# Fewer, smaller products for k and v, and the edits that came with them, in a one-core RWKV and routed-FFN layer

## The chip, the core and the metric

The kernel runs on one core of a Trainium2 chip. The metric is the device time of one execution in microseconds (us). The engines are named as the profile names them: PE is TensorE (its weight loads are PEld), DVE is VectorE, ACT is ScalarE, POOL is GpSimd, SP is SyncE, which only starts DMAs here. Each engine runs its own instructions in the order in which they were issued; semaphores make one wait for another.

## The reference

```python
xn = layernorm(x)                                  # x: [1, 2048, 512]
r, v, k = split(xn @ W_rvk.T)                      # three of [2048, 512]
# per channel, w = -exp(time_decay), u = time_first, over the tokens in order:
#   no = max(o, u+k);  A = exp(o-no);  B = exp(u+k-no);  y = (A*p + B*v) / (A*q + B)
#   no2 = max(w+o, k); p, q, o = exp(w+o-no2)*p + exp(k-no2)*v, exp(w+o-no2)*q + exp(k-no2), no2
attn = (sigmoid(r) * y) @ W_out.T
probs = softmax(xn @ classifier.T)                 # 12 experts: 8 routed, 4 that return their input
idx = top_2(probs + bias);  w_full = one_hot(idx) * probs * 1.5
ffn = sum over e < 8 of w_full[e] * down_e(silu(gate_e xn) * up_e xn)  +  xn * sum of w_full[8:]
out = x + attn + ffn
```

All of it is fp32. gate and up are [256, 512] for each expert, down is [512, 256].

## The kernel before

Tokens are handled in 4 blocks of 512 (`NTB`, `TB`), channels in 4 chunks of 128 (`CC`). A block and a chunk, (b, c), make a unit, 16 in all.

**The head.** For each block the tokens are normalized (`norm`), stored to HBM as `xs`, turned by PE into `xnT` with channels on the partitions (`turn_block`), and multiplied by the classifier (`logits`, `add_quarters`). Then DVE works through the routing: it picks the two experts of each token, counts tokens per expert with one-hot matmuls (`pc`), gives each a slot in one of 23 tiles of 128 tokens (two of which mix experts in groups of 32), and builds one-hot tables in bf16: `lowhot` (L548, the place within a tile), `hh` (L555, the tile) and `tok` (L562, `hh` times the five values carried for each token). 32 matmuls of these tables (`pi`, L570) give the list of tokens and weights of every tile. While DVE does that, `fill(n)` issues n product steps on PE; before the tables these are 9 and 18, between the two halves 7, after them 2, 3, 4 and 5. The tables and all routing buffers stay allocated to the end of the kernel.

**The products.** `project(b, c)` (L270 to L291) computes k, v and r of a unit in turn: four fp32 matmuls of 128 x 128 by 128 x 512 each into one PSUM buffer of `ps_mm` (two buffers), one step per matmul; then ACT copies k or v to SBUF (L289), or takes exp of -r (L287). The first two units (`all_products`) go name by name.

**The recurrence.** `scan(b, c)` (L293 to L336) has four stages. Stage 0, DVE: the first column of `obv` from the state (L304), a running maximum (L308), two differences (L310, L311). Stage 1, ACT: two exponentials (L313, L314). Stage 2, DVE: two running sums and a product (L320 to L322), then numerator and denominator (L326 to L329). Stage 3: POOL copies the last column of `obv` into the channel's state (L332), ACT that of `sums` (L333), DVE takes the reciprocal (L334) and multiplies into `yT` (L335). The buffers `obv` and `a2` come from `wk`, which has two of each; `sums` and `den` from `wk1`, with one.

**The expert tiles.** For tile i POOL gathers 128 rows of `xs` (`gather`, L642); `flip` copies them on ACT as 16-bit halves (L709), a DMA on SP's queue transposes them, `unite` puts the halves together on ACT (L717); `turn` (L697) is the other way, four PE transposes and one ACT copy, used only for tiles beyond the 23. Then gate and up on PE (`up`), tanh on ACT and two DVE operations (`activate`), the turned activation, the down product (`finish`) into `ps_o`, scaled by ACT into `yo` (L770), and a scatter on POOL's queue that adds the 128 rows to `out` in HBM (L774). Each such accumulating DMA waits until the one before has landed. SP fetches the weights (1 MB for gate and up, 0.5 MB for down).

**The attention output.** `attention(b, [j])` multiplies 128 tokens of `yT` by W_out (L875), into `ps_tr` for the first rows; DVE adds the share of the input-returning experts (L887), and POOL's queue adds the row block to `out` (L890). The last blocks go through `read_out` instead, which reads `out` back, adds (L845, L884, L871) and stores.

**The order.** After the head the order is a table: `plan(at, generator)` gives each step a due time in nominal microseconds, and the steps are issued in order of due time. Units of the recurrence are planned every `UNIT` = 19.0, with stages at 0, 4, 6 and 12; product steps in groups of four; `after` names the groups in whose place a piece of attention stands; a tile has a first half (up, activate, gather of the tile after next but one) and a second half. The very end is the attention of the last two blocks.

Of the kernel before, what the change touches and what calls it, by code (L numbers as in the profile page):

```python
# [26 lines left out]
F32 = mybir.dt.float32  # L27
BF16 = mybir.dt.bfloat16
I32 = mybir.dt.int32
U16 = mybir.dt.uint16  # L30
AF = mybir.ActivationFunctionType
# [4 lines left out]
P = 128  # L36
T = 2048
C = 512
# [17 lines left out]
MAX_TILES = 40  # L56
FAR = 8192.0
NV = 5
QW = 32


@with_exitstack
def layer(ctx: ExitStack, tc: tile.TileContext, x, w_rvk, w_out, decay, first, cls, ebias, gu, down, out):
    nc = tc.nc

    def pool(name, bufs, **kw):
        return ctx.enter_context(tc.tile_pool(name=name, bufs=bufs, **kw))
# [3 lines left out]
    xyp = pool("xy", 5)  # L71
    ewp = pool("ew", 3)
    gathered = pool("gathered", 2)
    wk1 = pool("wk1", 1)
    rows = pool("rows", 3)
    basep = pool("base", 4)
    rp = pool("route", 1)
    small = pool("small", 2)
    kvp = pool("kv", 5)
    erp = pool("er", 4)  # L80
    wk = pool("wk", 2)
    ex_p = pool("exp", 2)
    dram = pool("dram", 1, space=bass.MemoryType.DRAM)
    ps_mm = pool("ps_mm", 2, space=bass.MemoryType.PSUM)
    ps_gu = pool("ps_gu", 2, space=bass.MemoryType.PSUM)
    ps_o = pool("ps_o", 2, space=bass.MemoryType.PSUM)
    ps_tr = pool("ps_tr", 2, space=bass.MemoryType.PSUM)

    xs = dram.tile([T, C], F32, tag="xs", name="xs")

# [77 lines left out]
        nc.gpsimd.tensor_copy(t, i32)  # L168
        return t

    lane = iota([P], [[1, P]], 0, "lane", BF16)
    tiles128 = iota([MAX_TILES], [[P, MAX_TILES]], 0, "tiles128", BF16)
    tiles_f = iota([MAX_TILES], [[P, MAX_TILES]], 0, "tiles_f", F32)
    number = iota([MIXED], [[1, MIXED]], 0, "number", F32, 1)
    expert = iota([E], [[1, E]], 0, "expert", F32)
    tok_j = iota([2, NT], [[0, 2], [1, NT]], 0, "tok_j", BF16, 1)
    tok_p = iota([1], [[0, 1]], 1, "tok_p", F32)
    spare = iota([2], [[0, 2]], 1, "spare", F32, T + P)
    vals = rp.tile([P, 2, NT, NV], BF16, tag="vals", name="vals")
    nc.gpsimd.tensor_copy(vals[:, :, :, 0], tok_j)  # L180
    nc.gpsimd.tensor_copy(vals[:, :, :, 1], tok_p.unsqueeze(1).to_broadcast([P, 2, NT]))
    one8 = rp.tile([P, E], F32, tag="one8", name="one8")
    nc.gpsimd.memset(one8, 1.0)
    hotb = rp.tile([P, NT + 1, E], BF16, tag="hotb", name="hotb")
# [108 lines left out]
    def scan(b, c):  # L293

        n = f"{b}_{c}"
        s = state[c]
        w, cf = wdec[:, c : c + 1], cfac[:, c : c + 1]
        k = kvr[b, c, "k"]
        if c == 0:
            yT[b] = xyp.tile([P, CC, TB], F32, tag="xy", name=f"yT{b}")  # L300


        obv = wk.tile([P, 3, TB + 1], F32, tag="obv", name=f"obv{n}")
        nc.vector.tensor_copy(obv[:, :, 0:1], s[:, 0:3].unsqueeze(2))  # L304
        o, bs, bvs = (obv[:, m, 0:TB] for m in range(3))
        o2, b2, bv = (obv[:, m, 1 : TB + 1] for m in range(3))

        nc.vector.tensor_tensor_scan(o2, w.to_broadcast([P, TB]), k, s[:, 0:1], ALU.add, ALU.max)  # L308
        a2 = wk.tile([P, TB], F32, tag="a2", name=f"a2{n}")
        nc.vector.scalar_tensor_tensor(a2, o, w, o2, ALU.add, ALU.subtract)  # L310
        nc.vector.tensor_sub(b2, k, o2)  # L311
        yield
        nc.scalar.activation(a2, a2, AF.Exp)  # L313
        nc.scalar.activation(b2, b2, AF.Exp)  # L314
        yield

        v = kvr[b, c, "v"]
        sums = wk1.tile([P, 2, TB], F32, tag="sums", name=f"sums{n}")
        sq, sp = sums[:, 0, :], sums[:, 1, :]
        nc.vector.tensor_tensor_scan(sq, bs, a2, s[:, 3:4], ALU.add, ALU.mult)  # L320
        nc.vector.tensor_mul(bv, b2, v)
        nc.vector.tensor_tensor_scan(sp, bvs, a2, s[:, 4:5], ALU.add, ALU.mult)  # L322

        er = kvr[b, c, "r"]
        den = wk1.tile([P, TB], F32, tag="den", name=f"den{n}")
        nc.vector.scalar_tensor_tensor(den, b2, cf, sq, ALU.mult, ALU.add)  # L326
        nc.vector.scalar_tensor_tensor(den, er, 1.0, den, ALU.add, ALU.mult)
        num = wk.tile([P, TB], F32, tag="a2", name=f"num{n}")
        nc.vector.scalar_tensor_tensor(num, bv, cf, sp, ALU.mult, ALU.add)  # L329
        yield  # L330
        if b + 1 < NTB:
            nc.gpsimd.tensor_copy(s[:, 0:3].unsqueeze(2), obv[:, :, TB : TB + 1])  # L332
            nc.scalar.copy(s[:, 3:5].unsqueeze(2), sums[:, :, TB - 1 : TB])  # L333
        nc.vector.reciprocal(den, den)  # L334
        nc.vector.tensor_mul(yT[b][:, c, :], num, den)  # L335
        yield  # L336

    units = [(b, c) for b in range(NTB) for c in range(CC)]
    LEAD = 4

    def whole(gen):
        for _ in gen:
# [1 line left out]

    def all_products():
        for name, m in (("k", 2), ("v", 1), ("r", 0)):
            for u in range(2):
                yield from project(*units[u], ((name, m),))
        for u in range(2, len(units)):
            yield from project(*units[u])  # L350

    products = all_products()

    def fill(n):
        for _ in range(n):
            next(products, None)


    manual = ExitStack()
    manual.enter_context(tc.manual_schedule())  # L360
# [7 lines left out]
    for b in range(NTB):  # L368
        if b + 1 < NTB:
            norm(b + 1)  # L370
        fill(1 if b else 2)
        logits(b)
        fill(1 if b else 3)
        if b + 1 < NTB:
            turn_block(b + 1)
        add_quarters(b)
# [73 lines left out]
    nc.vector.tensor_reduce(wts, hot[:, :, :, :E], AX.X, ALU.add)  # L450
    nc.vector.tensor_scalar_mul(wts, wts, 0.5 * SCALE)

    for n in range(3):
        nc.vector.tensor_copy(vals[:, :, :, 2 + n], wts)
        if n < 2:
            nc.vector.tensor_sub(wts, wts, vals[:, :, :, 2 + n])

    def narrow8(tag, dt=F32):
        return rp.tile([P, E], dt, tag=tag, name=tag)

# [77 lines left out]


    NK = 2 * NT
    lowhot = xyp.tile([P, NK, P], BF16, tag="xy", name="lowhot")
    pi = ps_o.tile([P, NV, MAX_TILES], F32, tag="o", name="pi")
    fill(18)
    for m in range(2):
        ks = slice(m * NT, (m + 1) * NT)
        nc.vector.tensor_tensor(  # L548
            lowhot[:, ks, :],
            lane.unsqueeze(1).to_broadcast([P, NT, P]),  # L550
            low[:, m].unsqueeze(2).to_broadcast([P, NT, P]),
            ALU.is_equal,
        )
        hh = rp.tile([P, NT, MAX_TILES], BF16, tag="hh", name=f"hh{m}")
        nc.vector.tensor_tensor(  # L555
            hh,
            tiles128.unsqueeze(1).to_broadcast([P, NT, MAX_TILES]),
            high_b[:, m].unsqueeze(2).to_broadcast([P, NT, MAX_TILES]),
            ALU.is_equal,
        )  # L560
        tok = ewp.tile([P, NT, NV, MAX_TILES], BF16, tag="gw", name=f"tok{m}")
        nc.vector.tensor_tensor(  # L562
            tok,
            hh.unsqueeze(2).to_broadcast([P, NT, NV, MAX_TILES]),
            vals[:, m].unsqueeze(3).to_broadcast([P, NT, NV, MAX_TILES]),
            ALU.mult,
        )
        for j in range(NT):
            k = m * NT + j
            nc.tensor.matmul(pi, lowhot[:, k, :], tok[:, j], start=(k == 0), stop=(k == NK - 1))  # L570
        if m == 0:
            which_i = place_tiles()
            fill(7)
    nc.vector.tensor_scalar_mul(wdec, wdec, -1.0)
    cfac = const.tile([P, CC], F32, tag="cfac", name="cfac")
    nc.vector.tensor_add(cfac, first_sb, wdec)
# [272 lines left out]
    def attention(b, js=range(NJ)):  # L849

        for j in js:
            i = b * NJ + j
            if i < (NTB - 2) * NJ - 2:
                po = ps_tr.tile([P, C], F32, tag="tr", name=f"pw{i}")
            elif j >= 2 if i in orows else j % 2 == 1:
                po = ps_mm.tile([P, C], F32, tag="mm", name=f"pw{i}")
            else:
                po = ps_o.tile([P, C], F32, tag="o", name=f"pw{i}")
# [31 lines left out]
                nc.gpsimd.dma_start(out[i * P : (i + 1) * P, :], xrows[i], accum_op=ALU.add)  # L890


    gather(0)
    gather(1)
    for i in range(2):
# [1 line left out]
        fetch_down(i)  # L897
        fetched["w"] += 1
        fetched["d"] += 1
    fill(2)  # L900
    stages = [scan(*u) for u in units]
    next(stages[0])
    fill(3)
    next(stages[0])
    fill(4)
    next(stages[0])
    flip(0)
    flip(1)
    fill(5)
    next(stages[0])  # L910
    gather(2)
    unite(0)

    UNIT = 19.0
    after = {12: (0, 0), 13: (0, 1), 18: (0, 2), 19: (0, 3), 32: (1, 0), 33: (1, 1), 40: (1, 2), 41: (1, 3)}
    groups = 3 * (len(units) - LEAD) - 2 + len(after)  # L920
    total = groups * 3.43 + TILES * 5.2
    table = []

    def plan(at, what, *args):
        table.append((at, iter([(what, *args)]) if args else what))

    for u in range(1, len(units)):
        for at in (0, 4, 6, 12):
            plan((u - 1) * UNIT - 7 + at, stages[u])
    one = total / groups / CC  # L930
    for m in range(groups):
        if m in after:
            b, j = after[m]
            group = attention(b, [j])
            plan(CC * m * one - 16, read_xn, b, [j])

            plan(CC * (m + 2 - j % 2) * one + 1, group)
        else:
            group = products
        for k in range(CC):  # L940
            plan((CC * m + k) * one, group)


    spread = (total - 12) / TILES
# [83 lines left out]
```

## Time and profile before

| | |
|---|---|
| median of 3 runs | 379.0 us (377.15 to 381.65) |
| profiled execution | 379.6 us, span 377.8 us |
| PE busy | 369.5 us, 98% |
| DVE busy | 273.2 us, 72% |
| ACT, POOL busy | 161.4 us (43%), 95.3 us (25%) |
| granted PE clock, mean | 0.995 |
| DMA | 87.37 MB, mean 231 GB/s |

The page divides the span into 40 slices; each digit is the busy share of an engine in tenths, 9 standing for 90% or more. A row of groups has line, engine, operation, out<-in, sizes, count, then busy us, mean ns of one, and the idle time of the engine just before such instructions with what ended it. Matmuls are pipelined, and each record contains the fill of the array, so records overlap and busy PE time is less than the sum of the records. An fp32 matmul leaves two matmul records and two weight loads. A line of the timeline has start, duration, engine, line and operation; the bracket at its end is the idle time before it and what ended that.

The head's fixed points in the timeline: the last logits at 37.3, counts `pc` at 45.1, `lowhot` from 54.62, the first `tok` until 61.2, `pi` until 70.2, the token list at 71.24, the first expert product at 85.6. PE's last matmul ends at 374.27.

### The profile page before, as it was taken

To read this page: it belongs to the slowest core of one execution; us is meant where nothing else is said; L and a number is where in the kernel's file an instruction comes from. 1 tells how busy PE (TensorE), PEld (TensorE's weight loads), DVE (VectorE), ACT (ScalarE), POOL (GpSimd) and SP (SyncE) were. 2 spreads that over 40 slices of the span, in tenths; PEclk is the share of its full clock that TensorE was granted. 3 is DMA by queue.
4 is the path that set the end of the run, shared out by engine and by line. 5 is a ranking of instruction groups with operands and counts; after the bars stand their busy time and mean duration, and the time that the engine had idled before them with its cause. 6 is when DMAs were issued, how large, how long until landed. Compare 5 with 4: busy or idle time off the path is not lost. (4 is left out here: it accounts for less than half of the span.)

```text
span 377.8 us, 3672 instructions
## 1 busy us (share of the span) xinstructions
PE 369.5 (98%) x1076; PEld 167.0 (44%) x1076; DVE 273.2 (72%) x420; ACT 161.4 (43%) x266; POOL 95.3 (25%) x131
## 2 busy tenths in 40 slices
PE   7999999999999999999999999999999999999996
PEld 2565444534443443434434444444444444434443
DVE  4872889899995887556957685929593779379905
ACT  1676211153455555535454655445642644432000
POOL 5000300231123322221332333424122311322520
PEclk9899999999999999999999999999999999999999
DMA  7998941835878799999999899799999698774494
GB/s 275 404 360 303 334 141 61 320 77 157 177 214 222 164 335 282 314 271 316 240 208 302 236 244 289 158 248 356 209 246 267 154 320 165 155 249 56 58 205 158
DMA packets 59605, 87.37 MB, mean 231 GB/s; under 512 B 38976, under 2 KB 39360, under 8 KB 55808
## 3 DMA queue, kind: packets, MB, share of 16 engines
q1 hardware_dynamic: 52272, 67.07, 59.8%
q0 software_dynamic: 7312, 20.06, 24.7%
q8 instruction: 9, 0.15, 0.2%
q14 instruction: 12, 0.10, 0.1%
HBM read 63.25 MB, written 19.27 MB: 218 GB/s over the span
## 5 line engine op out<-in xcount | busy, mean ns | idle before, releaser
L684 PE MATMUL pg<-gw,xgT 128*128 128x512 f32 x168 | 75.8, 593 | 0.0
L774 POOL DMA_INDIRECT out_dram<-yo,to_i x23 | 39.0, 1697 | 133.9 <-ACT yo L770 55.8
L276 PE MATMUL pk<-xnT,wrvk 128*128 128x512 f32 x128 | 60.7, 598 | 0.5 <-ACT v L289 0.5
L276 PE MATMUL pr<-xnT,wrvk 128*128 128x512 f32 x128 | 59.8, 593 | 0.0
L276 PE MATMUL pv<-xnT,wrvk 128*128 128x512 f32 x128 | 59.6, 596 | 0.0
L875 PE MATMUL pw<-wout_sb,yT 128*128 128x512 f32 x120 | 54.0, 594 | 0.1
L334 DVE RECIPROCAL den<-den 128x512 f32<-128x512 f32 x16 | 53.5, 3345 | 0.0
L684 PEld LDWEIGHTS pg<-gw,xgT 128*128 128x128 f32 x168 | 31.8, 190 | 40.1 <-issue 37.5
L736 DVE SCALAR_TENSOR_TENSOR th<-th,pg 128x256 f32<-128x256 f32 x23 | 9.6, 419 | 54.8 <-ACT th L735 54.8
L684 PE MATMUL po<-dw,actT 128*128 128x512 f32 x84 | 39.6, 593 | 0.8 <-ACT yo L770 0.8
L276 PEld LDWEIGHTS pv<-xnT,wrvk 128*128 128x128 f32 x128 | 23.9, 190 | 30.7 <-issue 29.2
L276 PEld LDWEIGHTS pk<-xnT,wrvk 128*128 128x128 f32 x128 | 23.9, 192 | 30.6 <-issue 29.1
L276 PEld LDWEIGHTS pr<-xnT,wrvk 128*128 128x128 f32 x128 | 24.1, 190 | 30.0 <-issue 29.5
L875 PEld LDWEIGHTS pw<-wout_sb,yT 128*128 128x128 f32 x120 | 22.6, 190 | 28.6 <-issue 28.6
L642 POOL DMA_INDIRECT xg<-xs,token_i x23 | 24.4, 1059 | 40.3 <-DMA gw<-in_gu_dram 30.2
L735 ACT ACTIVATE th<-pg 128x256 f32<-128x256 f32 x23 | 8.8, 383 | 54.0 <-PE pg L684 46.7
L320 DVE TENSOR_TENSOR_SCAN sums<-obv,state,a 128x512 f32<-128x512 f32 x16 | 20.5, 1282 | 12.8 <-ACT obv L314 12.8
L709 ACT COPY xp<-xg 128x1024 uint16<-128x1024 uint16 x23 | 24.0, 1045 | 6.7 <-DMA xq<-xp 3.7
L717 ACT COPY xgT<-xq 128x1024 uint16<-128x1024 uint16 x23 | 26.7, 1159 | 0.0
L684 PEld LDWEIGHTS po<-dw,actT 128*128 128x128 f32 x84 | 15.9, 190 | 21.2 <-issue 19.1
L770 ACT ACTIVATE yo<-po,wplace 128x512 f32<-128x512 f32 x23 | 15.8, 685 | 19.5 <-PE po L684 19.4
L322 DVE TENSOR_TENSOR_SCAN sums<-obv,state,a 128x512 f32<-128x512 f32 x16 | 20.6, 1284 | 0.6
(195 smaller groups left out, 389.9 us busy)
## 6 DMA issues: line engine op xcount, KB each, us to landing
gw<-in_gu_dram SPq DMA_DIRECT2D x25, 1024.0 KB, 7.9
dw<-in_down_dram SPq DMA_DIRECT2D x25, 512.0 KB, 4.5
x<-in_x_dram SPq DMA_DIRECT2D x16, 256.0 KB, 5.4
xs<-x SPq DMA_DIRECT2D x16, 256.0 KB, 4.4
wrvk<-in_w_rvk_dram SPq DMA_DIRECT2D x3, 1024.0 KB, 7.2
xrow<-xs SPq DMA_DIRECT2D x8, 256.0 KB, 4.6
out_dram<-xrow POOLq DMA_DIRECT2D x8, 256.0 KB, 8.1
xrows<-xs SPq DMA_DIRECT2D x8, 256.0 KB, 5.3
```

Of the source, the lines that this page charges most:

```text
L276: nc.tensor.matmul(ps, wrvk_sb[m][:, k, c * P : (c + 1) * P], xnT[b][:, k, :], start=(k == 0), stop=(k == CC - 1),)
L320: nc.vector.tensor_tensor_scan(sq, bs, a2, s[:, 3:4], ALU.add, ALU.mult)
L322: nc.vector.tensor_tensor_scan(sp, bvs, a2, s[:, 4:5], ALU.add, ALU.mult)
L334: nc.vector.reciprocal(den, den)
L642: nc.gpsimd.indirect_dma_start(out=xg, out_offset=None, in_=xs, in_offset=bass.IndirectOffsetOnAxis(ap=token[:, column(i) : column(i) + 1] ...
L684: nc.tensor.matmul(out_, lhs[:, c, :], rhs[0][:, c, :], start=(c == 0), stop=(c == last))
L709: nc.scalar.copy(xp, st[i]["xg"].bitcast(U16).rearrange("p (c h) -> p h c", h=2))
L717: nc.scalar.copy(xgT.bitcast(U16).rearrange("p c (t h) -> p c t h", h=2), st[i]["xq"].rearrange("p (h c) t -> p c t h", h=2),)
L736: nc.vector.scalar_tensor_tensor(th, th, 1.0, pg[:, 0, :], ALU.add, ALU.mult)
L770: nc.scalar.activation(yo, po, AF.Identity, scale=weight[:, column(i) : column(i) + 1])
L774: nc.gpsimd.indirect_dma_start(out=out, out_offset=bass.IndirectOffsetOnAxis(ap=index, axis=0), in_=yo[ps], in_offset=None, compute_op=ALU ...
L875: nc.tensor.matmul(po, yT[b][:, c, j * P : (j + 1) * P], wout_sb[:, c, :], start=(c == 0), stop=(c == CC - 1),)
```

## The change

- **Seven products.** For all units but the first two, `seven(b, c)` computes k and v together. The contraction is split into two halves of 256 channels and the block into two halves of 256 tokens, and [k; v] is then a 2 x 2 by 2 x 2 block product, done with seven half-size products in place of eight (Strassen's scheme in Winograd's form). r stays as it was. Eleven steps for each unit in place of twelve. The sums of token halves S1 to S4 (once a block), of weights T2 to T4 (once) and the in-place difference of two weight halves are DVE's. Four of the products (M1, M6, M7, M4) accumulate in one PSUM buffer, and ACT copies it out between them; M5 and M3 share another, M2 has a third. What must be added afterwards is queued in `owed` and done by DVE.
- **Tables in pairs.** The one-hot tables get an innermost dimension of two contiguous bf16 elements, in all operands. They live in the buffers of the experts' weights; `place_tiles` moves behind both halves. The fills become 9, 16, 2, 4, 4.
- **The first tile** is turned by PE (`turn(0)`); the flip of tile 1 and the gather of tile 2 enter the table.
- **The recurrence's buffers**: `obv` and `a2` single; `den` and `num` written in place of `sq` and `a2`; the state of the sums copied by DVE in stage 2, that of `obv` still by POOL in stage 3. The routing pool is closed ahead of the steady part, and `wk1` and `ex_p` take its space.
- **The plan**: `UNIT` 17.6, `LEAD` 2, other offsets, the groups of `after` one earlier, the last step of each piece of attention planned one group on; `pw` of the first rows in `ps_o`.

```diff
-        obv = wk.tile([P, 3, TB + 1], F32, tag="obv", name=f"obv{n}")
+        obv = wk1.tile([P, 3, TB + 1], F32, tag="obv", name=f"obv{n}")
-        a2 = wk.tile([P, TB], F32, tag="a2", name=f"a2{n}")
+        a2 = wk1.tile([P, TB], F32, tag="a2", name=f"a2{n}")
...
-        den = wk1.tile([P, TB], F32, tag="den", name=f"den{n}")
+        den, num = sq, a2
+        if b + 1 < NTB:
+            nc.vector.tensor_copy(s[:, 3:5].unsqueeze(2), sums[:, :, TB - 1 : TB])
...
             nc.gpsimd.tensor_copy(s[:, 0:3].unsqueeze(2), obv[:, :, TB : TB + 1])
-            nc.scalar.copy(s[:, 3:5].unsqueeze(2), sums[:, :, TB - 1 : TB])
...
+    def sum_weights():
+        for n in (2, 3, 4):
+            wsum[n] = sump.tile([P, 2, C], F32, tag=f"T{n}", name=f"T{n}")
+        nc.vector.tensor_sub(wsum[3], weights(1, 1), weights(1, 0))
+        nc.vector.tensor_add(wsum[2], wsum[3], weights(2, 0))
+        nc.vector.tensor_sub(wsum[4], weights(2, 1), wsum[2])
...
+    def sum_tokens(b, n):
...
+        if n == 1:
+            nc.vector.tensor_add(S[1], part(b, 0, 1), part(b, 1, 1))
+        elif n == 2:
+            nc.vector.tensor_sub(S[2], S[1], part(b, 0, 0))
+        elif n == 3:
+            nc.vector.tensor_sub(S[3], part(b, 0, 0), part(b, 0, 1))
+        else:
+            nc.vector.tensor_sub(S[4], part(b, 1, 0), S[2])
...
+        def multiply(ps, m, begin, end):
+            a, w = factors(b, m)
+            for k in range(2):
+                nc.tensor.matmul(
+                    ps[:, :HALF],
+                    w[:, k, cs],
+                    a[:, k, :],
+                    start=(begin and k == 0),
+                    stop=(end and k == 1),
+                    skip_group_check=True,
+                )
...
+        p1 = bank(ps_mm, "mm", "p1_")
+        multiply(p1, 1, True, False)
+        k = place(kvp, "k")
+        nc.scalar.copy(k[:, :HALF], p1[:, :HALF])
+        yield
+        pr = bank(ps_tr, "tr", "pr")
+        r_step(0)
+        yield
+        emit_owed()
+        r_step(1)
+        yield
+        multiply(p1, 6, False, False)
+        v = place(kvp, "v")
+        nc.scalar.copy(v[:, :HALF], p1[:, :HALF])
+        yield
+        p3 = bank(ps_mm, "mm", "p3_")
+        multiply(p3, 5, True, False)
+        m5 = five.tile([P, HALF], F32, tag="m5", name=f"m5_{n}")
+        nc.scalar.copy(m5, p3[:, :HALF])
+        yield
+        p2 = bank(ps_tr, "tr", "p2_")
+        multiply(p2, 2, True, True)
+        owed.append(lambda: add(k[:, :HALF], p2[:, :HALF]))
+        next_sums((1, 2))
+        yield
+        multiply(p1, 7, False, False)
+        nc.scalar.copy(v[:, HALF:], p1[:, :HALF])
+        next_sums((3,))
+        yield
+        r_step(2)
+        emit_owed()
+        yield
+        r_step(3)
+        r = place(erp, "r")
+        nc.scalar.activation(r, pr, AF.Exp, scale=-1.0)
+        yield
+        multiply(p1, 4, False, True)
+        nc.scalar.copy(k[:, HALF:], p1[:, :HALF])
+        yield
+        multiply(p3, 3, False, True)
+        owed.append(lambda: add(v[:, :HALF], p3[:, :HALF]))
+        owed.append(lambda: add(v[:, HALF:], m5))
+        next_sums((4,))
+        yield
...
-    lowhot = xyp.tile([P, NK, P], BF16, tag="xy", name="lowhot")
...
-    fill(18)
+    fill(16)
...
+    lowhot = ewp.tile([P, NK // 2, P, 2], BF16, tag="gw", name="lowhot")
...
         nc.vector.tensor_tensor(
-            lowhot[:, ks, :],
-            lane.unsqueeze(1).to_broadcast([P, NT, P]),
-            low[:, m].unsqueeze(2).to_broadcast([P, NT, P]),
+            lowhot[:, ks],
+            lane.unsqueeze(1).to_broadcast([P, H, P, 2]),
+            in_pairs(low, m).unsqueeze(2).to_broadcast([P, H, P, 2]),
             ALU.is_equal,
         )
...
-            which_i = place_tiles()
-            fill(7)
+            fill(2)
+    which_i = place_tiles()
+    emit(3)
...
-                po = ps_tr.tile([P, C], F32, tag="tr", name=f"pw{i}")
+                po = ps_o.tile([P, C], F32, tag="o", name=f"pw{i}")
...
-    fill(2)
+    fill(4)
+    emit(1)
     stages = [scan(*u) for u in units]
     next(stages[0])
-    fill(3)
-    next(stages[0])
+    emit(2)
     fill(4)
-    next(stages[0])
-    flip(0)
-    flip(1)
-    fill(5)
-    next(stages[0])
-    gather(2)
-    unite(0)
+    turn(0)
+    emit(1)
...
-    UNIT = 19.0
-    after = {12: (0, 0), 13: (0, 1), 18: (0, 2), 19: (0, 3), 32: (1, 0), 33: (1, 1), 40: (1, 2), 41: (1, 3)}
+    UNIT = 17.6
+    after = {11: (0, 0), 12: (0, 1), 17: (0, 2), 18: (0, 3), 31: (1, 0), 32: (1, 1), 39: (1, 2), 40: (1, 3)}
...
+    for at in (0, 3, 9):
+        plan(at, stages[0])
     for u in range(1, len(units)):
         for at in (0, 4, 6, 12):
-            plan((u - 1) * UNIT - 7 + at, stages[u])
+            plan((u - 1) * UNIT + 10 + at, stages[u])
+    plan(2, flip, 1)
+    plan(3, gather, 2)
...
-            plan(CC * (m + 2 - j % 2) * one + 1, group)
+            plan(CC * (m + 1) * one + 1, group)
```

## The prediction

> **What bounds the kernel now.** I read the summary and slices of the page first, then the chain that ended last, then groups by line, and last the timelines of TensorE (PE) and GpSimd (POOL).
>
> ```profile
> PE 369.5 (98%) x1076; PEld 167.0 (44%) x1076; DVE 273.2 (72%) x420; ACT 161.4 (43%) x266; POOL 95.3 (25%) x131
> ...
> PE   7999999999999999999999999999999999999996
> ...
> DVE  4872889899995887556957685929593779379905
> ...
> PE 3%; DVE 0%; issue 0%
> PE pw L875 2%; PE pw_last L863 0%; PE pw L863 0%; DVE orows L871 0%
> ```
>
> PE is busy in every slice, and the end is a chain of PE work with one VectorE (DVE) add behind it. In the steady part PE waits only 0.49 us (before k at L276, for ACT's v at L289) and 0.78 us (before po, for ACT's yo at L770). So a microsecond of PE work taken out is a microsecond gained, provided PE goes on finding its inputs ready. DVE has 28% free, but it is 8 and 9 tenths busy in slices 5 to 12, the routing stage.
>
> **What the product costs.** An fp32 matmul is two records here. The first two lines are PE's timeline (start, duration, count), the others group rows:
>
> ```profile
> 343.64 19.90 PE L875 MATMUL pw<-wout_sb,yT 128*128 128x512 f32 x46
> 372.36 1.89 PE L863 MATMUL pw_last<-wout_sb,yT 128*128 128x256 f32 x8
> ...
> L276 PE MATMUL pk<-xnT,wrvk 128*128 128x512 f32 x128 | 60.7, 598 | 0.5 <-ACT v L289 0.5
> L863 PE MATMUL pw_last<-wout_sb,yT 128*128 128x256 f32 x8 | 1.9, 379 | 0.0
> L863 PEld LDWEIGHTS pw_last<-wout_sb,yT 128*128 128x128 f32 x8 | 1.5, 190 | 0.2
> ```
>
> The mean of one (598, 379) contains the fill of the array; what counts is the pitch. 512 columns: (19.90 − 0.59)/45 = 0.429 us. 256 columns: (1.89 − 0.379)/7 = 0.216 us, half, with a weight load of 0.190 just hidden inside it.
>
> **What the Trainium skill says.** "VectorE: DVE Perf Modes", the perf-mode tier table: a bf16 tensor_tensor of 2048 elements takes 1224 ns if all operands have step 1, and 2293 ns otherwise. Before's `lowhot`, with a broadcast innermost, took 2288 ns: it agrees with the slow figure; no run here shows the fast one. "Vector Engine (DVE) Microarchitecture Reference", section 5.1: a repeated single element runs at 1x, while innermost rows of two elements do run in the packed mode. That is the form of the new tables. "PSUM — Partial Sum Buffer", engine vs sequencer instructions: ScalarE (ACT), DVE and GpSimd queues are strict FIFO, PE's matmuls start and finish in order. POOL's timeline below agrees.
>
> **The change, part by part.**
>
> *Seven products.* 14 units lose 8 matmuls of 512 columns (k and v, 16 passes x 0.429 = 6.86 us) and get 7 x 2 of 256 (28 passes x 0.216 = 6.04). 14 x 0.82 = **−11.5 us of PE**. Bounds: with exactly half a pass −12.0; if the load came out of hiding by 0.02 a pass (392 passes), −3.7. I take −11.5, as L863 shows that load under that pass.
>
> *What it costs DVE.* Per unit three adds of 256: two read PSUM (L871: 0.42), one SBUF (between 0.34, half of L321's 0.67, and 0.42; I take 0.36): 14 x 1.2 = 16.8. Sums of tokens, 4 blocks x 4 x 0.67 (row L321, the same size) = 10.7. Sums of weights, 4 of 1024 elements: at L321's rate and L548's (2048 in 2.29) about 1.2 each = 4.8. State copies moved from ACT, 12 x 0.16 (L304) = 1.9. DVE then has 273.2 + 34.2 − 6.6 (below) = 301 us; per unit of the steady part about 16 of the planned 17.6. That is room on average, without slack for a late start. ACT copies five halves (about 0.37 each, L746) for two of 0.58: 14 x 0.7 = +10 to about 171 of 370, no bound.
>
> *Tables in pairs.*
>
> ```profile
> L562 DVE TENSOR_TENSOR tok<-hh,vals 128x3200 bf16<-128x3200 bf16 x2 | 7.0, 3492 | 0.1
> L548 DVE TENSOR_TENSOR lowhot<-lane,low 128x2048 bf16<-128x2048 bf16 x2 | 4.6, 2288 | 0.0
> L555 DVE TENSOR_TENSOR hh<-tiles,high_b 128x640 bf16<-128x640 bf16 x2 | 1.6, 818 | 0.0
> ```
>
> 13.2 us become about 6.6. This buys no time by itself, since product steps cover it in both kernels: after needs only 16 + 2 of them (now of 0.86 us) where before has 18 + 7. I placed the new order on before's times: `lowhot` starts 1.2 later (the in-place weight sum ahead of it), the first table ends near 59.2 against PE at 59.6, the second near 62.6 against 62.7. So 0. If packing fails (upper bound), DVE ends 6.6 us later and PE, out of planned steps, waits that long. The block sums (6 us) go under DVE's 7.4 us wait for the logits.
>
> *First tile turned by PE.* Four transposes, +0.6 us. The gather is issued near 66.7 and the four products and r steps behind it end at 71; gathers here landed in 3.4 to 6.8 us. PE waits 0 to 3; I take 1.2. What goes is one flip and one unite on ACT, beside PE anyway: 0.
>
> *PSUM and the halves.* p1 accumulates M1, M6, M7 and M4 with an ACT copy between, p3 needs the DVE add of the unit before. Following PE's, ACT's and DVE's new orders with the durations above, these waits stay: M5 of (1,0) 0.8; M1 of (1,1) 0.7; M5 of (1,1), behind stage 2 of a scan on DVE, 2.0 to 3.4 (2.7); `pw`, now in ps_o, behind ACT's yo 0.9; M3 of (3,0) 0.6. With the gather 6.9. Bounds: 1 (if everything on ACT and DVE starts 2 us sooner than in my replay) and 10. Before's 0.49 goes.
>
> *Single recurrence buffers.* `obv` exists once. Stage 0 of a unit on DVE now waits until POOL has copied the last column of the unit before (L332), and POOL's queue is FIFO, with scatters that wait for each other's landing. What is queued behind that stage on DVE is the adds, and for those PE waits (M5). Before's POOL timeline, with what each waited for in brackets:
>
> ```profile
> 215.37 1.58 POOL L774 DMA_INDIRECT out_dram<-yo,to_i  x1 [5.82 <-ACT obv L314]
> 217.26 1.01 POOL L642 DMA_INDIRECT xg<-xs,token_i  x1 [0.30 <-issue]
> 220.60 1.87 POOL L890 DMA_DIRECT2D out_dram<-xrow  x2 [2.34 <-DVE num L329]
> 231.74 1.61 POOL L774 DMA_INDIRECT out_dram<-yo,to_i  x1 [9.27 <-DMA out_dram<-xrow]
> 233.65 1.03 POOL L642 DMA_INDIRECT xg<-xs,token_i  x1 [0.30 <-DVE th L736]
> 234.67 1.10 POOL L332 COPY state<-obv 128x3 f32<-128x3 f32 x1
> ```
>
> That copy ran at 234.67; DVE had begun its next unit at 226.53. With one buffer DVE would have stood 8 to 9 us. Three of the twelve copies were late (by 5, 8 and about 1). In the new order the tightest place is (2,0), after (1,3): PE has 73 to 74 us of work from po of tile 3 to M5 of (2,2), while POOL's chain (scatters of tiles 3 to 8, two late ones, four adds of rows no longer all in pairs) has some ten links of 6 to 8 us, the copy coming 66 to 80 us after po, and 3.1 us of stage 0 and add stand behind it. PE's wait is 0 to 10. In the forecast I take 0, the links at the short end (scatters measured 5.9, 6.3, 6.7); the long end is rival A. POOL itself gets no more work.
>
> *Tail.* The last units' yT is ready about 4 us before PE asks for it (before about 5): 0.
>
> **Sum**, against the profiled execution, 379.6 us (span 377.8 and 1.8 around it): −11.5 + 0.6 + 6.9 − 0.5 = −4.5, so 375.1. That run lay 0.6 above the median of 379.0 (runs 377.15 to 381.65): **forecast 374.5**, 1.2% faster.
>
> **Rivals.**
>
> *A, slower: POOL's state copy decides.* With links at their mean, (5.9 + 9.25 + 6.7 + 7.6 + 6.3 + 10.2 + 8.7 + 5.9 + 7.0)/9 = 7.5, the copy comes near 79 after po, the add near 82, and PE stands 8 to 10 us before M5 of (2,2), with a shorter one elsewhere. 374.5 + 10 = **384.5**. It is slower than before by over 1% once PE's wait there exceeds 8.3. For it: the measured lateness. Against: short links are as common.
>
> *B, faster: the waits close up.* If M5's and the gather's waits shrink to 1 in all, −11.5 + 0.6 + 1 − 0.5 = −10.4: **368.5**. For it: DVE and ACT have 18 and 50% free; against: order, not load, makes these waits.
>
> *C, slower: the packing does not take hold, or DVE becomes the bound.* 6.6 us of wait in the routing stage, 374.5 + 6.6 = 381; with part of A, up to 388. I put it at **383**. For it: no run shows the packed form; against: the skill's section names it.
>
> **Chances.** Forecast 0.40 (371 to 378), A 0.32 (379 to 389), B 0.17 (366 to 371), C 0.11. What a measurement of this kernel can tell from no change is about 1%, 375.2 to 382.8. Forecast gives 0.28 faster and 0.12 same, B all faster, A 0.06 same and 0.26 slower, C 0.03 and 0.08: faster 0.45, same 0.21, slower 0.34. Range 367 to 386, leaving out the low end of B and the top of A and C; the forecast's own range is 371 to 378.
>
> **What would show it.** PE busy near 359 us; passes of 256 columns in the new product line at a pitch of 0.216 where they stand in unbroken rows; `lowhot` at about 1.2 us; no idle before pi; a PE wait for DVE's add and a DVE wait for POOL's state copy at (2,0), small or large, which parts the forecast from A; DVE busy near 301. The prediction is wrong if weight loads widen the 256-column pitch, if PE's waits on p1 and p3 recur in each unit instead of at a few, or if the scatters' landings move.

## The result, and the profile after

The changed kernel took 410.1 us (median of 4 runs, 408.7 to 416.3) against 379.9 us before (4 runs): 1.079 times as long, 95% interval 1.070 to 1.088. The run of 416.3 us was a slow execution, and the ratio leaves it out. The forecast, 374.5 us with a range of 367 to 386, was wrong in sign and in range. The profiled execution spans 409.0 us, 31.2 more than before. Its page:

```profile
PE 366.6 (90%) x1248; PEld 201.3 (49%) x1248; DVE 299.1 (73%) x494; ACT 166.4 (41%) x295; POOL 92.4 (23%) x131
...
PE   7999998896999999999994099999999598699996
...
PEclk9999999899999999999999589999999989899999
```

PE is busy 2.9 us less than before, where the working had 10.9 less, and it now has holes, the deepest in slices 10, 22, 23, 32 and 35. PE idles 42.4 us in the span (before 8.3), of which 35.4 are waits after the head (before 1.3, the two that the prediction names). The row of granted clock has holes at or just behind most of these. So the ledger is +34.1 idle − 2.9 busy = +31.2. PE's last matmul ends at 404.95 (before 374.27), so nearly all of the loss arises before that. The waits of PE and then of DVE, summed over the span (total, times, longest):

```profile
PE p L406 <- DVE v L416: 26.1, 4, 14.9
PE px L866 <- DMA xg<-xs,token_i: 3.6, 1, 3.6
PE po L849 <- issue: 2.3, 2, 1.8
PE p L406 <- ACT k L465: 1.1, 1, 1.1
...
DVE th L901 <- ACT th L900: 43.6, 15, 7.7
DVE obv L307 <- POOL state L336: 21.0, 3, 16.3
```

In these names p is a buffer of the seven products, pg holds gate and up of a tile, po its down product, pw a row block of attention, px the first tile's transposes, and xgT a tile's turned rows. Three quarters of PE's idle time after the head is one line: M5 waiting for the DVE addition that empties p3. The longest of the four, 14.9 us, is followed here through three engines' timelines, PE first:

```profile
218.52 1.03 PE L406 MATMUL p<-S,T 128*128 128x256 f32 x4
234.45 2.07 PE L406 MATMUL p<-S,wrvk 128*128 128x256 f32 x4 [14.90 <-DVE v L416]
236.31 1.63 PE L406 MATMUL p<-xnT,wrvk 128*128 128x256 f32 x4
```

Then DVE:

```profile
214.35 0.69 DVE L338 TENSOR_TENSOR yT<-a,sums 128x512 f32<-128x512 f32 x1
231.32 0.17 DVE L307 COPY obv<-state 128x3 f32<-128x3 f32 x1 [16.27 <-POOL state L336]
...
233.98 0.41 DVE L416 TENSOR_TENSOR v<-v,p 128x256 f32<-128x256 f32 x1
```

And POOL:

```profile
143.98 1.70 POOL L939 DMA_INDIRECT out_dram<-yo,to_i  x1 [7.51 <-ACT yo L935]
...
178.36 1.58 POOL L939 DMA_INDIRECT out_dram<-yo,to_i  x1 [9.03 <-ACT xgT L882]
...
191.47 1.81 POOL L939 DMA_INDIRECT out_dram<-yo,to_i  x1 [10.00 <-ACT xgT L882]
...
198.94 1.47 POOL L939 DMA_INDIRECT out_dram<-yo,to_i  x1 [4.34 <-DVE act L903]
...
207.48 1.57 POOL L939 DMA_INDIRECT out_dram<-yo,late_i  x1 [5.70 <-DMA out_dram<-yo,to_i]
214.76 0.95 POOL L1055 DMA_DIRECT2D out_dram<-xrow  x1 [5.70 <-DVE sums L337]
223.55 1.59 POOL L939 DMA_INDIRECT out_dram<-yo,to_i  x1 [7.84 <-DMA out_dram<-xrow]
228.81 0.91 POOL L1055 DMA_DIRECT2D out_dram<-xrow  x1 [3.67 <-DMA out_dram<-yo,to_i]
230.03 1.06 POOL L807 DMA_INDIRECT xg<-xs,token_i  x1 [0.30 <-issue]
231.06 0.23 POOL L336 COPY state<-obv 128x3 f32<-128x3 f32 x1
```

A copy of 0.23 us stands behind a queue of accumulating DMAs, and from 198.94 on each of them was issued only after the one before had landed. Some brackets name another engine, but the trace has the landings: 190.72 ahead of the issue at 191.47, 214.22 ahead of 214.76. DVE cannot begin unit (2,0), the addition behind it cannot run, and PE, which needs p3 for M5 of (2,2), stops. This is the place that rival A named. The four passes after the idle take 2.07 us where four passes in a row take 1.03: the clock is at half. The other M5 waits stand at 99.1 (3.5 us), 326.2 (4.6) and 350.7 (3.1), with no late copy by POOL near them. These groups show the two new prices; the four M groups have 112, 112, 112 and 56 records of the same work:

```profile
L406 PE MATMUL p<-S,wrvk 128*128 128x256 f32 x112 | 32.0, 412 | 26.2 <-DVE v L416 26.1
L406 PE MATMUL p<-S,T 128*128 128x256 f32 x112 | 28.8, 379 | 0.0
...
L707 DVE TENSOR_TENSOR lowhot<-lane,low 128x2048 bf16<-128x2048 bf16 x2 | 2.4, 1223 | 0.0
```

The group that no wait touches has a mean of 379 ns, as L863 had before; the one behind the waits has 412. The table in pairs takes 1.223 us instead of 2.288.

### The profile page after: what moved, and what is told of

The parts are those of the page before. It is cut to its first block, busy times and chain, and to the rows that moved or that the text cites. A ratio compares the mean times of both kernels' runs of the same rounds, so it can differ in the third digit from the quotient of the medians.

```text
span 409.0 us, 4109 instructions
## 1 busy us (share of the span) xinstructions
PE 366.6 (90%) x1248; PEld 201.3 (49%) x1248; DVE 299.1 (73%) x494; ACT 166.4 (41%) x295; POOL 92.4 (23%) x131
## 5 line engine op out<-in xcount | busy, mean ns | idle before, releaser
L406 PE MATMUL p<-S,wrvk 128*128 128x256 f32 x112 | 32.0, 412 | 26.2 <-DVE v L416 26.1
L419 PE MATMUL pr<-xnT,wrvk 128*128 128x512 f32 x112 | 54.4, 600 | 0.0
L337 DVE RECIPROCAL sums<-sums 128x512 f32<-128x512 f32 x16 | 53.5, 3344 | 0.0
L406 PEld LDWEIGHTS p<-S,wrvk 128*128 128x128 f32 x112 | 22.3, 204 | 33.4 <-DVE v L416 28.2
L406 PE MATMUL p<-xnT,wrvk 128*128 128x256 f32 x112 | 30.4, 396 | 1.2 <-ACT k L465 1.1
L419 PEld LDWEIGHTS pr<-xnT,wrvk 128*128 128x128 f32 x112 | 21.5, 194 | 19.4 <-issue 18.2
L323 DVE TENSOR_TENSOR_SCAN sums<-obv,state,a 128x512 f32<-128x512 f32 x16 | 20.5, 1282 | 13.2 <-ACT obv L317 13.2
L406 PE MATMUL p<-S,T 128*128 128x256 f32 x112 | 28.8, 379 | 0.0
L406 PEld LDWEIGHTS p<-xnT,wrvk 128*128 128x128 f32 x112 | 22.2, 200 | 9.0 <-issue 4.1
L406 PEld LDWEIGHTS p<-S,T 128*128 128x128 f32 x112 | 21.2, 190 | 9.3 <-issue 6.2
```

Source lines behind the costliest of these rows:

```text
L406: nc.tensor.matmul(ps[:, :HALF], w[:, k, cs], a[:, k, :], start=(begin and k == 0), stop=(end and k == 1), skip_group_check=True,)
L419: nc.tensor.matmul(pr, wrvk_sb[0][:, k, cs], xnT[b][:, k, :], start=(k == 0), stop=(k == CC - 1))
```

## The experiments

The theory formed from the two traces (1): POOL's late copy stops DVE, and DVE's queue stops PE. Its rival (2): DVE's queue is too tightly coupled to PE's by p3 in any case, and POOL only makes the first large hole. Versions were timed in five sets, each with executions of before beside them, whose medians were 378.1 to 379.3 us. Where no interval stands, the time is one execution, and a difference of 1% says little.

### POOL's copy moved to DVE, everything else as changed

```diff
-            nc.gpsimd.tensor_copy(s[:, 0:3].unsqueeze(2), obv[:, :, TB : TB + 1])
+            nc.vector.tensor_copy(s[:, 0:3].unsqueeze(2), obv[:, :, TB : TB + 1])
```

> The changed kernel, but DVE instead of POOL copies the last column of obv into the state. Theory 1 (POOL's late state copy stops DVE, and DVE's queued adds stop PE): the 14.9 us wait before M5 at 219.5 goes and the slow PE clock after it, about 5 us more, and the late passes near 326 in part: 380 to 390 us. Theory 2 (DVE is too tightly packed for the adds anyway, POOL only shows it first): the waits for DVE's adds come back elsewhere, 400 us or more.

405.7 us, 1.068 (1.059 to 1.077) times before; this interval overlaps that of the changed kernel. Theory 1 in its simple form fell: the 14.9 us wait is gone, and other waits came in its place. PE's waits:

```profile
PE p L406 <- DVE v L416: 15.1, 5, 4.6
PE p L406 <- ACT k L465: 5.1, 2, 3.9
PE px L866 <- DMA xg<-xs,token_i: 3.5, 1, 3.5
```

With the copy out of the way DVE still reaches its additions late, five times. At 324 us, for instance, DVE had waited 9.4 us for a tile's tanh, because PE's product for that tile stands behind attention products in PE's own order; then it had stage 2 and stage 3 of a unit and a row of attention, 9.8 us, to do before the addition that PE wanted:

```profile
312.99 0.42 DVE L901 SCALAR_TENSOR_TENSOR th<-th,pg 128x256 f32<-128x256 f32 x1 [9.36 <-ACT th L900]
...
319.58 3.34 DVE L337 RECIPROCAL sums<-sums 128x512 f32<-128x512 f32 x1
...
323.56 0.41 DVE L416 TENSOR_TENSOR v<-v,p 128x256 f32<-128x256 f32 x1
```

### The additions left out

The three additions that complete k and v of a unit are left out, so k and v are incomplete.

```diff
-        owed.append(lambda: add(k[:, :HALF], p2[:, :HALF]))
-        owed.append(lambda: add(v[:, :HALF], p3[:, :HALF]))
-        owed.append(lambda: add(v[:, HALF:], m5))
```

> The changed kernel without the three DVE additions per unit that complete k and v, so k and v lack those parts. Theory 1 and 2: PE's waits for v L416 (26 us) go, PE busy near 359, while DVE still waits about 16 us for POOL's state copy: 370 to 382 us, the end perhaps set by DVE or by POOL's chain of adds to out. If PE's waits come from the products' own PSUM copies on ACT: over 395 us.

380.2 us: 30 less than the changed kernel. No M5 waits. DVE still waits 13.7 us once for POOL's copy, and PE meets it another way: one idle of 6.6 us before a tile's product, for ACT's xgT, which stands on ACT behind an exponential that waits for DVE. So 30 us hang on the additions, which DVE is also spared here, and POOL's copy can reach PE without them.

### The kernel before with one obv

```diff
-        obv = wk.tile([P, 3, TB + 1], F32, tag="obv", name=f"obv{n}")
+        obv = wk1.tile([P, 3, TB + 1], F32, tag="obv", name=f"obv{n}")
```

> The kernel before with obv in one buffer and nothing else. Theory 1: DVE stops some 8 us at about 226, waiting for POOL's state copy, but no product waits for a DVE add here, so PE goes on: 377 to 383 us. Rival: DVE's lateness alone reaches PE through the buffers of k, v and r: 385 us or more.

380.1 us beside 378.2. DVE waits for POOL's copy twice, 16.4 us in all and up to 9.8 at once, much as the timeline of before had said it would (8 to 9). PE idles 1.6 us for it. So the single buffer makes DVE late in the old order too, but a late DVE costs PE little where the products do not wait for its additions.

### Eight products, the rest as changed

```diff
-            yield from seven(*units[u])
+            yield from project(*units[u])
...
-    fill(4)
+    fill(6)
     turn(0)
...
-    UNIT = 17.6
-    after = {11: (0, 0), 12: (0, 1), 17: (0, 2), 18: (0, 3), 31: (1, 0), 32: (1, 1), 39: (1, 2), 40: (1, 3)}
+    UNIT = 18.5
+    after = {12: (0, 0), 13: (0, 1), 18: (0, 2), 19: (0, 3), 33: (1, 0), 34: (1, 1), 42: (1, 2), 43: (1, 3)}
```

> The changed kernel with eight products (the old product routine) for all units, and so without adds and sums; tables in pairs, first tile turned by PE, single recurrence buffers stay, the plan is stretched to UNIT 18.5 and the groups of attention shifted. Theory 1 and 2: DVE may wait for POOL, PE does not: 378 to 388 us. If the single buffers or the plan by themselves cost PE: 395 us or more.

389.9 us. With the old products, and so neither additions nor sums, the other edits cost some 12 us: 7.2 us of PE idle at 228 (for ACT's xgT, behind POOL's copy by way of DVE and ACT) with half clock until 231.1, and 2.6 before po, with none. Three runs take this apart. First the state copy by DVE, as above:

> The eight-product variant of the changed kernel with the state copy by DVE. It showed one PE idle of 7.2 us and slow clock after it, behind POOL's copy by way of DVE and ACT: without POOL 376 to 381 us. If that idle has another cause: 386 us or more.

383.8 us, where I had expected 376 to 381. The idle of 7.2 is 1.1 now; 2.7 us before po remain, here with half clock behind them. Then the attention rows go back from ps_o to ps_tr, and their planned additions are adjacent again:

```diff
-                po = ps_o.tile([P, C], F32, tag="o", name=f"pw{i}")
+                po = ps_tr.tile([P, C], F32, tag="tr", name=f"pw{i}")
...
-            plan(CC * (m + 1) * one + 1, group)
+            plan(CC * (m + 2 - j % 2) * one + 1, group)
```

> The eight-product variant with the state copy by DVE, and the attention rows back in ps_tr with the additions of a pair of rows next to each other as before. If the 2.7 us that PE stood before po, and the slow clock behind it, come from rows in ps_o: 377 to 380 us, as the kernel before. If they come from the plan: 383 us.

375.9 us, and no PE idle at all after the head. A row in ps_o holds the bank that the next tile's po needs until DVE has added it: in the two runs before, that addition ended at 296.70 and 290.03, and po began at 296.81 and 290.13. What the order of the additions did beside the bank, this run does not part. With these rows but POOL's copy:

> Eight products, rows in ps_tr in pairs, but the state copy by POOL. If the copy alone stops PE in single buffers: about 10 us over its twin with DVE's copy, 384 to 388 us. If the long queue (rows not in pairs) made the copy late: 376 to 380 us.

378.9 us. DVE waits 2.6 us in all for the state, PE has no idle after the head; 2.6 of the 3 us over the run before arise in the head (the last matmul of `pc` starts at 46.77 against 44.15), where the first transposes came later and at a slow clock (2.78 us for 13 where the other run had 1.64). So with the rows back in ps_tr and in pairs DVE waits at most 1.5 us for POOL's copy, where it waited 9.0 with the rows in ps_o, and the copy costs next to nothing: the single buffer by itself was not the fault.

### ACT empties p3

Back to seven products. ACT copies M5 + M3 to SBUF and DVE adds from there, so PE's next M5 waits for ACT alone.

```diff
-        owed.append(lambda: add(v[:, :HALF], p3[:, :HALF]))
+        s3 = sump.tile([P, HALF], F32, tag="s3", name=f"s3_{n}")
+        nc.scalar.copy(s3, p3[:, :HALF])
+        owed.append(lambda: add(v[:, :HALF], s3))
```

> The changed kernel, but ACT copies M5+M3 out of PSUM into SBUF and DVE adds from there, so PE's next M5 waits for ACT and no more for DVE's queue. If the waits for v L416 (26 us with their slow clock more) are what costs: 380 to 388 us, with DVE still stopped some 14 us by POOL's state copy and PE caught by it elsewhere for about 7. If waits only change their name: 400 us or more.

390.1 us, 20 less than the changed kernel, by a single copy of 0.4 us per unit. All four M5 waits are gone. DVE still does the same additions. That decides for theory 2 on the larger part. POOL's copy is still late (DVE waits 14.9 us at once) and PE meets it through ACT. PE's timeline there:

```profile
230.48 6.42 PE L851 MATMUL pg<-gw,xgT 128*128 128x512 f32 x8 [8.44 <-ACT xgT L884]
```

With the copy by DVE as well:

> The run before and the state copy by DVE together. If the two couplings (PE on DVE's adds, DVE on POOL's copy) are the whole loss: 366 to 375 us, faster than the kernel before. If DVE or ACT has become too full for the order: 385 us or more.

387.8 us, 1.024 (1.018 to 1.029) times before. I had expected 366 to 375 us, or 385 and more if DVE or ACT had become too full. POOL's queue holds more than the copy: at 225.7 a gather came late, ACT stood 6.6 us for its rows, and the copy that empties p1 stood behind that on ACT:

```profile
234.18 1.13 PE L406 MATMUL p<-xnT,wrvk 128*128 128x256 f32 x4 [3.27 <-ACT k L465]
```

### Gathers earlier in POOL's queue

```diff
-        if i + 3 < n:
-            gather(i + 3)
+        if i == 0:
+            gather(3)
...
             flip(i + 2)
+        if i + 4 < n:
+            gather(i + 4)
         if i > 1:
             finish(i - 2)
```

> The same without the later turn of the first tile. The gather's wait before px stays (3.3 us and 1 to 2 us of slow clock), so 4 to 5 us above the run before; equal to it if that wait moves elsewhere.

378.5 us, 9 below its parent: the idles of 3.3 and 2.5 us are gone, and no half clock is granted after 8 us. Not all of the 9 belongs to the edit: 3.4 us of it is half clock that the parent's execution had in the head and behind its wait before px, where the edit changes nothing. The wait before px stayed, as expected. With the first tile turned three steps later (`plan(3.5, turn, 0)`):

> The variant with both couplings loosened (ACT empties M5+M3, state copy by DVE), and two more: each gather is issued half a tile earlier, ahead of the scatter in POOL's queue, and the first tile is turned three product steps later. Its parent lost 3.3 us before px with slow clock after it, and 3.3 and 2.5 us where ACT stood behind a late gather. If POOL's queue still sets these: 375 to 381 us. If gathers are late for want of a free buffer: 385 us or more.

377.4 us, 0.997 (0.994 to 1.000) times before: the wait before px fell from 3.0 to 0.2 us, but the gain over the run before is not resolved; I had expected 4 to 5 us. With POOL's copy instead of DVE's, gathers early, px as changed:

> Seven products, ACT empties M5+M3, gathers early, but the state copy by POOL; its twin with DVE's copy took 378.5 us. If the copy still comes late: 384 to 390 us, with a DVE wait of 10 us or more for the state near the unit (2,0) and a PE idle behind it. If the early gather was what mattered: 378 to 381 us.

386.3 us, 8 above its twin (3.2 of it half clock, some of it behind px, which the twin did not have). DVE waits 11.9 us for the state at 221.8, and PE 6.8 for ACT's xgT. So in the seven-product plan, which does not put rows' additions in pairs, POOL's copy is late whatever the gathers do. The same edit on the changed kernel alone:

> The changed kernel with nothing but the gathers issued half a tile earlier in POOL's queue. In the loosened variant that one edit took 9 us. If POOL's queue is the root, here too: 398 to 403 us, with the wait for the state copy near 220 shorter. If DVE's queue by itself stops PE through p3: 405 to 411 us.

405.7 us, the wait at M5 of (2,2) 8.8 instead of 14.9, the others nearly as they were: the range that I had expected if DVE's queue by itself stops PE through p3. And the version with early gathers and late turn, with its first attention rows in ps_gu:

```diff
-                po = ps_o.tile([P, C], F32, tag="o", name=f"pw{i}")
+                po = ps_gu.tile([P, C], F32, tag="gu", name=f"pw{i}")
```

> The variant with early gathers and late turn, and the first attention rows in ps_gu instead of ps_o. It stood 1.9 us before po because that bank still held a row that DVE had not added, with about 1 us of slow clock behind it. Gone: 373 to 376 us, faster than before by about 1%. If the rows now hold up pg in ps_gu: 377 us or more.

380.1 us, 1.004 (1.001 to 1.006): missed. The 1.9 us before po went, and a gate product waited 3.9 us for its bank in ps_gu, with half clock behind it.

### What beats both

Eight products with all the loosened edits (the one with rows back in ps_tr and the copy by DVE, and gathers early):

> Eight products, tables in pairs, first tile turned by PE, single buffers, state copy by DVE, rows in ps_tr in pairs, and gathers early. Its parent had no PE idle after the head and one time of 375.9 us. If the small edits are a gain by themselves: 374 to 377 us, 0.5 to 1% below the kernel before. If that was chance: 378 to 380 us.

376.0 us, 0.994 (0.993 to 0.996) times before, the best version here, and below both kernels. Its page:

```profile
PE 368.1 (98%) x1080; PEld 166.4 (45%) x1080; DVE 271.6 (73%) x444; ACT 158.4 (42%) x253; POOL 91.3 (24%) x119
```

It has no PE idle after the head, where before had 1.3 us. The seven products were not in it. Beside it the seven-product version with early gathers has 8.4 us less PE work, but 11.7 us of waits after the head: 3.3 for ACT's copies out of p1, 3.0 before px, 1.9 before po, the rest in waits of 1.3 us and less. Seven products with the rows in ps_tr and in pairs were not tried, nor were additions issued earlier in DVE's order, so no run says what seven products could give at best.

## Why the prediction was wrong

**The pitch and the work: nearly right.** 256-column passes in unbroken rows ran at 0.216 us (for instance starts 117.59, 118.45 and 119.31, four passes each), DVE was busy 299.1 us (worked out 301), ACT 166.4 (171), `lowhot` took 1.22 (1.2), so the packed form held, and PE did not wait for pi. In busy time the gain was smaller than the pitch says. The seven-product run with early gathers and the eight-product run that beats both have no half clock after 8 us, and PE busy from 8 us on of 352.8 and 361.2: 8.4 us for 14 units, not 11.5. The pitch itself was as forecast: 392 passes at 0.2155 us stand where 224 at 0.429 stood, 11.6 us less. Against that, the last pass before an idle is busy 0.16 us beyond its pitch and the first one behind it takes 0.1 us more, at nine idles some 2.5 us; 0.6 lies in smaller groups.

**The step that failed: PE's waits, sized at 6.9 us on p1, p3, `pw` and the gather (bound 10) and at 0 in the POOL term (up to 10).** Measured were 35.4 us, 20.5 and 14.9. The list of places was half right. Of the first term, the gather took 3.6 (forecast 1.2), M5 of (1,1) 3.5 (2.7), `pw` behind yo 0.8 (0.9); M5 of (1,0), M1 of (1,1) and M3 of (3,0) did not wait (0.8, 0.7, 0.6). Not on the list were M5 of (3,2) and (3,3) with 4.6 and 3.1, po behind rows in ps_o with 2.3, and three smaller ones with 2.7. What the replay had too early is DVE's addition, since it had too little in front of it in DVE's queue. Before the wait at 326.2 the queue stood 7.7 us for a tile's tanh, and then 10.6 us passed in the tile's own two operations, stages 2 and 3 of a unit and a row of attention:

```profile
315.13 0.42 DVE L901 SCALAR_TENSOR_TENSOR th<-th,pg 128x256 f32<-128x256 f32 x1 [7.66 <-ACT th L900]
...
325.70 0.41 DVE L416 TENSOR_TENSOR v<-v,p 128x256 f32<-128x256 f32 x1
```

That p3 is what carries this to PE is shown by the run in which ACT empties it: all four M5 waits went. That small waits earlier in the kernel brought the tanh and the additions into this order is likely, but not shown.

**The POOL term: right place, both sums too small.** The forecast took the short end of the links without a reason that the profile gave, and rival A's end was short too. The scatter of tile 3 is the one at 143.98; from there to the row at 228.81 the ten links (a row at 168.35 counted with the one 2.3 us ahead of it, for which it did not wait) took 84.8 us, 8.5 each instead of 6 to 8, the longest 13.1 (178.36 to 191.47). The copy came 90.1 us after po of tile 3 (141.0), where the working had 66 to 80 and rival A 79. PE's work up to M5 of (2,2) was longer as well, 78.6 us with 2.0 of waits in it, instead of 73 to 74; with the work as forecast the wait would have been near 20. Rival A came nearest (8 to 10), but only since its two errors partly cancel.

**The term that was not in the sum: the clock.** Half the clock after long idles was in no case. Weighting PE's busy time with the granted clock in windows of 1 us from 8 us on, the changed kernel lost 6.2 us to it, before 1.7, and the variant with the copy by DVE 13.4. That variant's windows around its wait of 3.2 us (stretch, length, PE busy, and after the engines the granted clock):

```profile
96.00:98.00 2.00, 1.29 (x5) 0.59 (x4) 1.90 (x4) 1.49 (x3) 0.61 (x1) 1.00 0.89 188
98.00:100.00 2.00, 0.00 (x0) 0.00 (x0) 1.97 (x3) 0.00 (x0) 0.47 (x1) 0.91 0.91 156
100.00:102.00 2.00, 1.53 (x4) 1.26 (x5) 2.00 (x5) 0.00 (x0) 0.00 (x0) 0.50 0.79 201
102.00:104.00 2.00, 2.00 (x6) 1.60 (x5) 2.00 (x1) 0.89 (x2) 0.00 (x0) 0.50 1.05 426
104.00:106.00 2.00, 2.00 (x4) 0.92 (x3) 0.78 (x2) 0.00 (x0) 0.00 (x0) 0.50 0.65 274
106.00:108.00 2.00, 2.00 (x5) 0.84 (x5) 0.00 (x0) 0.00 (x0) 0.00 (x0) 0.89 0.00 0
```

The idle of 3.2 us is followed by six us of work at half clock, which costs 3.0 us more, the dearest case here. In the changed kernel four idles (3.6, 14.9, 4.6 and 3.1 us) were followed by some 3 us of such work each, and so cost 1.4 to 1.7 us more each. The Trainium skill gives a rule in "TensorE: Matmul & The Clock Gate", HAM oscillation: no idle gaps of PE above about 3.4 us. The traces agree for long gaps: every idle of 3.6 us or more had half clock behind it. For shorter ones they do not show that limit: 1.9 us were enough twice (before po with POOL's copy by DVE, and with early gathers and late turn), 2.7 to 2.9 us four times, while 2.5, 2.6, 3.0, 3.3 and 3.5 us once each were not.

**The ledger.** PE work −8.4 by the pair of runs above, +0.6 px, +4.5 clock (6.2 − 1.7): −3.3, measured −2.9. Idle time +34.1.

**How the loss divides.** The first edits on the changed kernel, each alone, and each beside before in its own set: the changed kernel lies 30.2 us above it, with the additions away 1.9, with p3 emptied by ACT 10.8, with POOL's copy by DVE 27.4, with gathers early 27.1. The last two are too near to 30.2 to count as gains by themselves. The edits don't add up, since each opens the next wait. After p3, POOL's queue is the other part: its copy (6 to 8 us where gathers are early) and its gathers (5 to 6 us where the copy is DVE's, with the half clock taken off). Two obv buffers with seven products were not tried.

## What to carry to other kernels

A saving on a saturated engine counts only as far as that engine need not wait for work in another in-order queue: before moving work to an engine with 28% free time, list what stands in that queue ahead of each result that the saturated engine waits for, and empty PSUM by an engine whose own queue does not wait on late things. Price the half clock behind an expected PE idle of about 3 us and more too: in these traces it cost 1.4 to 3.0 us each time it came, whatever the length of the idle. And take a small copy on which another engine depends off a queue of waiting DMAs, or shorten that queue.

## What the runs showed that I had not expected

- Emptying one PSUM buffer by ACT instead of DVE, 0.4 us of work per unit, was worth 20 us; the wait it removed had a mean of 6.5 us in only four places.
- Moving gathers by half a tile, with no work changed, took away 5.8 us of PE idle in the loosened version; in the changed kernel, where p3 still couples PE to DVE, the gain was not clear of noise.
- The head varies with the clock: the same 13 transposes at about 11 us took 1.63 or 1.64 us in the traces of twelve versions and 2.8 to 3.0 in those of five. In the five PE had stood 1.3 to 2.2 us before the first transpose, in the twelve 1.1 or less.
- The edits around the seven products, once loosened, gave 0.6% by themselves; the best version with seven products, without the rows in pairs, 0.3%.
